# Four graph layers in one kernel: where the work at two layer borders is placed

## The chip, the cores and the metric

The kernel runs on one core of one Trainium2 chip. The metric is the device time of one execution in microseconds (us). Three runs of the kernel before took 2089.14, 2089.81 and 2091.94 us; their median, 2089.81 us, is the time before. A separate execution was recorded by the hardware profiler, and all durations of single instructions come from it.

The engines are called as the profile calls them: PE is TensorE (PEld its weight loads), ACT is ScalarE, DVE is VectorE, POOL is GpSimd, SP is SyncE. Each works through its own queue in order, and they wait for one another by semaphores.

## The reference

`x` has the shape (16, 1024, 64): 16 batches, 1024 nodes, 64 features. `adj` is a 1024 x 1024 graph that all batches and layers share. Four layers follow each other, each with a residual and a layer norm:

```python
x = layernorm(x + L0(x, W0, a0, adj))      # graph attention, one head
x = layernorm(x + L1(x, w0, b0, wa, ba, adj))
x = layernorm(x + L2(x, adj, W2, a2))      # graph attention, one head
x = layernorm(x + L3(x, adj, Wh, bh, Wo, bo, gamma, beta))   # dot-product attention, 4 heads and an outer one

# L0 and L2
h = x @ W;  s1 = h @ a1;  s2 = h @ a2
e = leaky_relu(s1[:, :, None] + s2[:, None, :], 0.2), masked by adj
out = elu(softmax(e, axis=2) @ h)

# L1: a softmax over the neighbours for each feature
feat = softplus(x * w0 / sqrt(2) + b0);  s = feat * wa + ba
out[i, d] = sum_j softmax_j(s[j, d], masked by adj[i, j]) * feat[j, d]
```

## The kernel before

The function `fast_path` does the work; `general_path` is a slower way that is run only if a test at the end of the data's range asks for it. The nodes lie on the 128 partitions, in 8 chunks; `xg[g]` holds four batches, so there are four groups g of four batches.

**Layers 0 and 2** are written by the same function, `gat_layer`. A pair of batches is prepared together: `prep_x` transposes x on PE (tile pxT) and copies it to SBUF on ACT (xT, line 920), `prep_s` multiplies it with w4 to the scores ps (line 926), `prep_top` copies them (l_s), takes their maximum on DVE (top) and over the partitions on POOL (gtop, line 937), `prep_p` makes two bounds (down, up) and two exponentials p and q on ACT, `prep_G` makes pg by matmuls (line 960) and its exponential G on ACT (line 961), and `prep_v` scales the values (vals) on ACT. Then a batch has eight units: one DVE instruction each makes e out of G, q and the graph aT (line 980), and PE multiplies e with vals (line 992; in layer 0 also line 1004, the sums u). A batch's ending is `evict` (yT, ysum), `project` (po, lines 1024 or 1032 and 1036), `divide` (v, and m = exp(v) at line 1061), `residual` (lines 1066, 1067), `norm` (statistics bn, line 1075, and for the second batch of a pair `moments`), `root`, `shift` and `store` (line 780). What belongs to which unit of which batch is written out by hand in `places` and `ends`; inside `gat_layer` the order of the instructions is the program's (`tc.manual_schedule`). The endings that fall past the last batch's fifth unit after the end are returned as a list, `ending`.

**Layer 1** works on groups. `prep_l1(g, q)` prepares half q of group g: the feature f and the exponent t on ACT and DVE, a transpose pf, a transpose back pe (line 1570), and hi and lo, the two halves of the exact product (lines 1572 to 1579: hi is a cast on ACT, lo the rest, on DVE). `product_l1` makes, for each of the eight chunks of nodes, 16 matmuls of aR (the graph, cast from aT at line 1666) with hi and lo into po, one PSUM bank of two (line 1642). `average` divides (lines 1652 to 1660: two steps on ACT, four on DVE) and takes statistics (line 1662). After a group's eight products come its moments; their root, shift and rows are put into the next group by the list `last`. Here the order is not fixed by hand: a scheduler orders each engine's queue when the kernel is built.

The two borders of the change are these. Between layers 0 and 1, a loop of four turns casts aR, finishes the halves of group 0 (`back` and `weighted` for both q), and puts the first three endings of layer 0's last batch into the turns:

```python
for i, task in enumerate([l1_tasks[q][-2 + i] for q in range(2) for i in range(2)]):
    for k in range(2 * i, 2 * i + 2):
        (nc.scalar.copy if k % 2 else nc.vector.tensor_copy)(aR[:, k, :], aT[:, k, :])
    for todo in [task] + ending[i : i + 1] * (i < 3):
        todo()
last = ending[3:]
```

Between layers 1 and 2, the pools of layer 1 are closed, layer 2's are opened, and the nine tasks that prepare layer 2's first pair (prep_x twice, prep_s twice, prep_top, prep_p, prep_G twice, prep_v) are called by `first` ahead of the first unit.

Of the kernel before, what the change touches and what calls it, by code (L numbers as in the profile page):

```python
# [8 lines left out]
F32 = mybir.dt.float32  # L9
# [3 lines left out]
AF = mybir.ActivationFunctionType  # L13
# [3 lines left out]
P = 128  # L17
FLT_MAX = 3.4028234e38
LN_EPS = 1e-5
ALPHA = 0.2  # L20
# [17 lines left out]
LAG = 2  # L38
# [544 lines left out]
def fast_path(  # L583
# [24 lines left out]
    nc = tc.nc  # L608
    B, N, D = x.shape
    C = N // P  # L610
# [4 lines left out]
    NG = B // GB  # L615
    HALF = N // 2
    CH = C // 2
# [58 lines left out]
    def catch_up():  # L676
        for task in [soon.pop(0) for _ in range(len(soon))]:
            task()
# [113 lines left out]
    def behind(step, lag):  # L792
        waiting.append(step)
        while len(waiting) > lag:
            waiting.pop(0)()

    def drain():
        while waiting:
            waiting.pop(0)()
# [97 lines left out]

        return [turn, scores] + [others, project] * zero_mean

    def gat_layer(w, name, zero_mean, extra, first, own, ordered):  # L900

        run = ExitStack()
        w1, w4, ind, s12, sums, w_out = (w[k] for k in ("w1", "w4", "ind", "s12", "sums", "out"))
        F = D - 1 if zero_mean else D
        pool = gp
        xT, G, pq, vals, only, stats = {}, {}, {}, {}, {}, {}
        if not zero_mean:
            ring = [pool.tile([P, C, 32], F32, tag=f"only{r}", name=f"only{r}", bufs=1) for r in range(3)]  # L910
            for t in ring:
                nc.gpsimd.memset(t, 0.0)

        def prep_x(b, h):
            if h == 0:
                xT[b] = pool.tile([P, N], F32, tag="xT", name=f"xT_{name}_{b}")
            pt = ps_t.tile([P, CH, P], F32, tag="t", name="pxT")
            for j in range(CH):
                nc.tensor.transpose(pt[:, j, :], x_pair(b, h * CH + j), ident)
            nc.scalar.copy(xT[b][:, h * HALF : (h + 1) * HALF], pt.rearrange("p j q -> p (j q)"))  # L920

        def prep_s(b, chunks):
            if 0 in chunks:
                pq[b] = ps_t.tile([P, HALF], F32, tag="t", name="ps12")
            for c in chunks:
                nc.tensor.matmul(
                    pq[b][:, 4 * c : 4 * c + 4], xT[b][:, c * P : (c + 1) * P], w4, start=True, stop=True
                )

        def prep_top(b):  # L930
# [19 lines left out]
            nc.scalar.activation(q, s2, AF.Exp, bias=up, scale=ALPHA - 1.0)  # L950
            pq[b] = (p, q, up)

        def prep_G(b, h):
            if h == 0:
                G[b] = pool.tile([P, 2, N], F32, tag="G", name=f"G_{name}_{b}")
            pg = ps_g.tile([P, 2, HALF], F32, tag="g", name="pg")
            cols = slice(h * HALF, (h + 1) * HALF)
            for i in range(2):
                rows = slice(i * D, (i + 1) * D)
                nc.tensor.matmul(pg[:, i, :], w1[rows, :], xT[b][rows, cols], start=True, stop=True)  # L960
            nc.scalar.activation(G[b][:, :, cols], pg, AF.Exp, bias=pq[b][2], scale=1.0 - ALPHA)  # L961

        def prep_v(b):
            p = pq[b - b % 2][0][:, :, b % 2]
            v = pool.tile([P, C, D], F32, tag="vals", name=f"vals_{name}_{b}", bufs=3)
            for c in range(C):
                nc.scalar.activation(v[:, c, :F], xb(b)[:, c, :F], AF.Copy, scale=p[:, c : c + 1])
            if zero_mean:
                nc.scalar.copy(v[:, :, F], p)
            else:  # L970
                only[b] = ring[b % 3]
                nc.scalar.copy(only[b][:, :, 0], p)
            vals[b] = v

        def attention(b):
            held = {}

            def unit(k):
                e = pool.tile([P, N], F32, tag="e", name="e", bufs=7 if zero_mean else 10)
                nc.vector.scalar_tensor_tensor(  # L980
                    e, G[b - b % 2][:, b % 2, :], pq[b - b % 2][1][:, k, b % 2 : b % 2 + 1], aT[:, k, :],
                    ALU.max, ALU.mult,
                )
                return e
# [24 lines left out]
            def evict():  # L1009
                y = ep.tile([P, HALF], F32, tag="y", name=f"yT_{name}_{b}")  # L1010
                nc.scalar.copy(y, held["y"])
                t = y
                if not zero_mean:
                    t = pool.tile([P, HALF], F32, tag="ysum", name=f"ysum_{name}_{b}")
                    nc.scalar.copy(t, held["t"])
                held["s"] = (y, t)

# [78 lines left out]
        slots = {}  # L1096

        def at(t, k, task):
            slots.setdefault((t, k), []).append(task)
# [15 lines left out]
        for b in range(0, B, 2):  # L1115
# [10 lines left out]
            for task, (t, k) in zip(chain, places):  # L1126
# [3 lines left out]
                    at(0, 0, task)  # L1130
                else:
                    ahead.append(task)
        for (t, k), todo in extra.items():
            for task in todo:
                at(t, k, task)
        first(ahead)
        if ordered:
            run.enter_context(tc.manual_schedule(engines=in_order))
        for t in range(B + 1):
            for k in range(C):  # L1140
                catch_up()
                if t < B:
                    unit, product, _ = work[t]
                    e = unit(k)
                    behind(lambda product=product, k=k, e=e: product(k, e), LAG if zero_mean else 2 * LAG)
                elif t == B and k == 0:
                    drain()
                if t < B or (t == B and k < own):
                    for task in slots.get((t, k), []):
                        task()  # L1150
        run.close()

        return [task for t in range(B, B + 3) for k in range(C) for task in slots.get((t, k), []) if (t, k) >= (B, own)]

# [431 lines left out]
    with tc.tile_pool(name="ps_g", bufs=1, space=bass.MemoryType.PSUM, reuse_waits="tile") as ps_g, tc.tile_pool(  # L1588
# [35 lines left out]
        for q, todo in enumerate(l1_tasks):  # L1624
            t = 7 + 2 * q
            places = (t, 0), (t, 2), (t, 4), (t, 6), (t + 2, 2), (t + 2, 7), (t + 3, 5)
            for place, task in zip(places, todo):
                extra.setdefault(place, []).append(task)
        ending = gat_layer(w_0, "l0", False, extra, first, 5, True)

    with tc.tile_pool(name="l1", bufs=2, reuse_waits="tile") as pool, tc.tile_pool(
        name="ps_l", bufs=2, space=bass.MemoryType.PSUM, reuse_waits="tile"
    ) as ps_l:
        l1["halves"] = pool
        l1["psum"] = lambda name: ps_l.tile([P, C, P], F32, tag="l", name=name)
        aR = pool.tile([P, C, N], F32R, tag="aR", name="aR", bufs=1)
# [12 lines left out]
        def average(g, ic, po, st):  # L1649
# [11 lines left out]
            for b in range(GB):  # L1661
                nc.vector.bn_stats(st[:, ic * GB + b, :], y[:, b, :])

        for i, task in enumerate([l1_tasks[q][-2 + i] for q in range(2) for i in range(2)]):
            for k in range(2 * i, 2 * i + 2):
                (nc.scalar.copy if k % 2 else nc.vector.tensor_copy)(aR[:, k, :], aT[:, k, :])
            for todo in [task] + ending[i : i + 1] * (i < 3):
                todo()
        last = ending[3:]
        for g in range(NG):  # L1670
            ahead = [[] for _ in range(C)]
            for q in range(2 if g + 1 < NG else 0):

                for ic, task in zip((q, q, q, q, q + 1, q + 2, q + 2, q + 4, q + 5), prep_l1(g + 1, q)):
                    ahead[ic].append(task)
            st = pool.tile([P, C * GB, 6], F32, tag="st1", name=f"st{g}")
            for ic in range(C):
                po = product_l1(g, ic)
                average(g, ic, po, st)
                for task in ahead[ic] + last[ic : ic + 1]:  # L1680
                    task()
            y = xg[g].rearrange("p c b d -> p (c b) d")
            mo = {}

            root, finish = moments(st)

            def shift(mo=mo, end=finish):
                mo["n"] = end()

            def rows(c, y=y, mo=mo):  # L1690
                scaled(y, y, mo["n"], range(c * 8, c * 8 + 8))

            last = [root, shift] + [lambda c=c, rows=rows: rows(c) for c in range(C * GB // 8)]
# [16 lines left out]
    def at(b, j, task, where=slots):  # L1710
        where.setdefault((b, j), []).append(task)
# [31 lines left out]
    for b in range(0, B, 2):  # L1743
        for t, j, task, where in (
# [14 lines left out]
            else:  # L1759
                at(b + t, j, task, where)  # L1760

    with tc.tile_pool(name="ps_g", bufs=1, space=bass.MemoryType.PSUM, reuse_waits="tile") as ps_g, tc.tile_pool(
        name="ps_p", bufs=1, space=bass.MemoryType.PSUM, reuse_waits="tile"
    ) as ps_p, tc.tile_pool(
        name="gat2", bufs=2, reuse_waits="tile"
    ) as gp:
        places = [(15, j) for j in (0, 1, 2, 3, 4, 5, 6, 7)]
        extra = {p: [task] for p, task in zip(places, ahead)}
        for p, task in zip(((0, 0), (0, 1), (0, 3), (0, 7), (1, 3), (1, 7)), last):
            extra.setdefault(p, []).append(task)  # L1770

        def first(ahead):
            for task in ahead:
                task()

        ending = gat_layer(later["w2"], "l2", True, extra, first, 5, True)
    for j, task in enumerate(ending):
        at(0, j, task)

# [125 lines left out]
```

## Time and profile before

| what | value |
|---|---|
| runs | 2089.14, 2089.81, 2091.94 us; median 2089.81 us |
| the profiled execution | 2090.28 us, of it the span from the first to the last instruction 2088.5 us |
| mean clock granted to TensorE | 0.977 of full speed |
| busy share of the span | PE 94%, DVE 87%, ACT 60%, PEld 41%, POOL 3% |
| layer 1's first product starts at | 295.63 us |
| layer 2's first unit starts at | 444.11 us |

Times inside the profile count from the span's start. A timeline's line has the start, the time, the engine, the line of the kernel with the operation, the written tile and the read ones, their shapes and the number of instructions taken together; in brackets stands how long the engine was idle before it and what ended that. A line of a group has busy time and mean ns, then the idle time ahead of the group's instructions and what ended most of it. A line of windows has, for a stretch of time, its length, each engine's busy time and instructions, the granted clock, the share of the DMA engines and GB/s.

### The profile page before, as it was taken

Reading aid. Unit: us, or ns where it says so; the run is one execution under the profiler, and the core shown is the slowest. Engines: PE = TensorE matmul, PEld = TensorE weight load, DVE = VectorE, ACT = ScalarE, POOL = GpSimd, SP = SyncE. Lnnn points to the kernel's source line nnn. Section 1 sums busy time; section 2 is a strip of 40 time slices with the busy share of each in tenths; the row PEclk is TensorE's granted clock in tenths of the full one; section 3 lists DMA queues with packets and bytes.
Section 4 is the critical chain, followed back from the end, with each engine's and each line's share of the span. In section 5 each row is a group of like instructions: output and inputs, shape, how many; then the busy total and the mean of one; then the engine's idle time right before and its main releaser. Section 6 shows DMA issues by size and latency. Waiting matters only on the chain.

```text
span 2088.5 us, 26441 instructions
## 1 busy us (share of the span) xinstructions
PE 1965.1 (94%) x10001; PEld 853.0 (41%) x10001; DVE 1820.0 (87%) x3197; ACT 1261.6 (60%) x2097; POOL 70.0 (3%) x77
## 2 busy tenths in 40 slices
PE   7999989998888999999999999999999999999983
PEld 4444347843332343334443434334343434433431
DVE  5899988879999777889898898988989989889997
ACT  4466568664556766566656656655665666665631
POOL 0000000000000000000000000000000000000001
PEclk9999999999999999999999999999999999999997
DMA  6000000000000200000000000000000000000000
GB/s 168 1 1 1 1 1 1 1 1 1 0 1 10 71 1 1 1 1 6 1 6 6 1 6 6 1 6 1 6 6 1 6 0 6 6 1 6 1 5 16
DMA packets 23655, 18.89 MB, mean 9 GB/s; under 512 B 19361, under 2 KB 19426, under 8 KB 23522
## 3 DMA queue, kind: packets, MB, share of 16 engines
q1 hardware_dynamic: 23218, 17.11, 2.8%
q8 instruction: 80, 1.31, 0.3%
q14 instruction: 53, 0.43, 0.1%
q10 hardware_dynamic: 304, 0.03, 0.0%
HBM read 12.95 MB, written 4.19 MB: 8 GB/s over the span
## 4 chain that ended last, share of the span: by engine, by line
PE 45%; DVE 39%; ACT 12%; issue 3%; SPq 0%; DMA 0%; POOL 0%; DVEq 0%; POOLq 0%; ACTq 0%
DVE e L1311 12%; PE y L1318 11%; PE s L1303 8%; DVE e L980 7%; ACT e L1307 6%; PE y_l L992 6%; DVE junk L1413 4%; PE po L1642 4%; DVE e L1424 4%; PE u_l L1004 3%; PE po L1333 2%; PE y L1433 2%; ACT e L1408 2%; DVE v L1343 2%; DVE z L786 1%
## 5 line engine op out<-in xcount | busy, mean ns | idle before, releaser
L1307 ACT ACTIVATE e<-s,shift 128x1024 f32<-128x1024 f32 x512 | 542.4, 1118 | 335.3 <-PE s L1303 334.4
L1311 DVE TENSOR_TENSOR e<-e,aT 128x1024 f32<-128x1024 f32 x512 | 600.4, 1217 | 1.9 <-ACT e L1307 1.8
L1318 PE MATMUL y<-e,vals 128*64 128x512 f32 x2048 | 490.0, 600 | 10.4 <-DVE e L1311 5.3
L1303 PE MATMUL s<-hT 64*128 64x512 f32 x2048 | 495.1, 603 | 1.2 <-ACT e L1307 0.9
L980 DVE SCALAR_TENSOR_TENSOR e<-G_l,q,aT 128x1024 f32<-128x1024 f32 x256 | 315.8, 1277 | 7.4 <-ACT G_l L961 7.3
L1303 PEld LDWEIGHTS s<-hT 64*128 64x128 f32 x2048 | 185.7, 186 | 278.0 <-issue 137.9
L992 PE MATMUL y_l<-e,vals_l 128*64 128x512 f32 x1024 | 262.8, 637 | 22.8 <-DVE e L980 22.0
L1318 PEld LDWEIGHTS y<-e,vals 128*64 128x64 f32 x2048 | 135.0, 137 | 277.4 <-issue 190.0
L1413 DVE SCALAR_TENSOR_TENSOR junk<-e,aN 128x1024 bf16<-128x1024 f32 x128 | 155.8, 1217 | 0.0
L1424 DVE TENSOR_TENSOR e<-e,aT 128x1024 f32<-128x1024 f32 x120 | 147.0, 1225 | 6.4
L1408 ACT ACTIVATE e<-s,shift 128x1024 f32<-128x1024 f32 x128 | 141.9, 1116 | 0.2 <-PE s L1403 0.2
L1403 PE MATMUL s<-h2T 64*128 64x512 f32 x512 | 130.7, 591 | 0.0
L992 PEld LDWEIGHTS y_l<-e,vals_l 128*64 128x64 f32 x1024 | 65.2, 142 | 160.4 <-issue 75.0
L1433 PE MATMUL y<-e,h2v 128*64 128x512 f32 x480 | 124.3, 596 | 0.7 <-DVE e L1424 0.7
L1642 PE MATMUL po<-hi,aR 128*128 128x512 f32 x256 | 102.8, 403 | 13.6 <-ACT hi L1578 8.6
L1642 PE MATMUL po<-lo,aR 128*128 128x512 f32 x256 | 101.2, 396 | 0.0
L780 ACT ACTIVATE x<-m,bn_shift,bn_rstd 128x64 f32<-128x64 f32 x256 | 88.5, 429 | 2.4 <-DVE bn_shift L771 2.4
L1246 POOL PARTITION_ALL_REDUCE gtop<-top x48 | 42.4, 884 | 1371.0 <-DVE top L1244 1269.2
L1333 PE MATMUL po<-wb,yT 128*128 128x130 f32 x512 | 74.2, 288 | 10.0 <-ACT e L1307 9.4
L1333 PEld LDWEIGHTS po<-wb,yT 128*128 128x128 f32 x512 | 61.9, 190 | 47.4 <-ACT e L1307 45.8
L1403 PEld LDWEIGHTS s<-h2T 64*128 64x128 f32 x512 | 49.9, 186 | 60.0 <-issue 27.4
L1337 DVE COPY sums<-po 128x8 f32<-128x8 f32 x64 | 10.8, 169 | 71.8 <-PE po L1333 71.8
(228 smaller groups left out, 2046.6 us busy)
## 6 DMA issues: line engine op xcount, KB each, us to landing
adj<-in_adj_dram SPq DMA_DIRECT2D x16, 512.0 KB, 4.1
x<-in_x_dram SPq DMA_DIRECT2D x16, 256.0 KB, 5.2
out_dram<-res SPq DMA_DIRECT2D x16, 256.0 KB, 2.0
wl<-in_L_gnn_Wh_dram SPq DMA_DIRECT2D x2, 64.0 KB, 3.4
wo<-in_L_gnn_Wo_dram SPq DMA_DIRECT2D x1, 64.0 KB, 3.0
l_wd<-in_L_gnn_W_dram ACTq DMA_DIRECT2D x2, 16.0 KB, 4.6
l_wd<-in_L_gnn_W_dram SPq DMA_DIRECT2D x2, 16.0 KB, 2.0
bo<-in_L_gnn_bo_dram SPq DMA_DIRECT2D x1, 32.0 KB, 3.0
```

The costliest lines, as they stand in the source:

```text
L980: nc.vector.scalar_tensor_tensor(e, G[b - b % 2][:, b % 2, :], pq[b - b % 2][1][:, k, b % 2 : b % 2 + 1], aT[:, k, :], ALU.max, ALU.mult,)
L992: nc.tensor.matmul(held["y"][h * D : (h + 1) * D, :], vals[b][:, k, :], e[:, h * HALF : (h + 1) * HALF], start=(k == 0), stop=(k == C - 1),)
L1303: nc.tensor.matmul(s[:, i, :], hT[rows, k * P : (k + 1) * P], hT[rows, cols], start=True, stop=True)
L1307: nc.scalar.activation(e, s, AF.Exp, bias=shifts[b, n])
L1311: nc.vector.tensor_tensor(e, e, bc_mid(aT[:, k, h * HALF : (h + 1) * HALF], 2), ALU.mult)
L1318: nc.tensor.matmul(held[h][i * D : (i + 1) * D, :], vals[b][:, k, :], e[:, i, :], start=(k == 0), stop=(k == C - 1),)
L1333: nc.tensor.matmul(o[:, j // 2, j % 2, :], held["y"][:, j * P : (j + 1) * P], wb[:, n, :], start=True, stop=True,)
L1403: nc.tensor.matmul(s[:, i, :], hT[rows, (i + k // CH) % 2, k % CH * P : (k % CH + 1) * P], hT[rows, 0, :], start=True, stop=True,)
L1408: nc.scalar.activation(e, s, AF.Exp, bias=shifts[b])
L1413: nc.vector.scalar_tensor_tensor(junk.rearrange("p c q -> p (c q)").bitcast(BF16), e.rearrange("p i q -> p (i q)"), 1.0, aN[:, k, :], ALU. ...
L1424: nc.vector.tensor_tensor(m, e, aT[:, k, :].rearrange("p (i q) -> p i q", i=2), ALU.mult)
L1642: nc.tensor.matmul(po.rearrange("p q k f -> p (q k f)"), aR[:, k, ic * P : (ic + 1) * P], e[:, k].rearrange("p q k f -> p (q k f)"), start ...
```

## The change

It has two parts.

At the border of layers 0 and 1, only layer 0's `project` is called ahead of the loop of four turns; `divide`, `residual` and what follows go into `last`, that is, into the tasks of group 0's eight products.

At the border of layers 1 and 2, the first pair's tasks are made ahead of layer 1. `prep_G` is split into `scores_G` (the matmuls) and `exps_G` (the exponentials). The first eight tasks (prep_x twice, prep_s twice, prep_top, prep_p, scores_G twice) are put into group 3 of layer 1, the last group; in place of layer 2's own tiles, xT takes two buffers of the pool ep (tag "v"), and pg layer 1's two PSUM buffers. The exponentials and vals are called when layer 1's SBUF pool is closed, and only then is its PSUM pool closed. Since the scheduler orders layer 1's queues, a task can land earlier than it is called.

```diff
-    def gat_layer(w, name, zero_mean, extra, first, own, ordered):
+    def gat_layer(w, name, zero_mean, own, room=None):
...
         def prep_x(b, h):
             if h == 0:
-                xT[b] = pool.tile([P, N], F32, tag="xT", name=f"xT_{name}_{b}")
+                if room and b == 0:
+                    xT[b] = room["xT"]()
+                else:
+                    t = gp.tile([P, N], F32, tag="xT", name=f"xT_{name}_{b}")
+                    xT[b] = [t[:, i * HALF : (i + 1) * HALF] for i in range(2)]
...
-        def prep_G(b, h):
-            if h == 0:
-                G[b] = pool.tile([P, 2, N], F32, tag="G", name=f"G_{name}_{b}")
-            pg = ps_g.tile([P, 2, HALF], F32, tag="g", name="pg")
-            cols = slice(h * HALF, (h + 1) * HALF)
+        def scores_G(b, h):
+            pg = room["g"]() if room and b == 0 else ps_g.tile([P, 2, HALF], F32, tag="g", name="pg")
             for i in range(2):
                 rows = slice(i * D, (i + 1) * D)
-                nc.tensor.matmul(pg[:, i, :], w1[rows, :], xT[b][rows, cols], start=True, stop=True)
-            nc.scalar.activation(G[b][:, :, cols], pg, AF.Exp, bias=pq[b][2], scale=1.0 - ALPHA)
+                nc.tensor.matmul(pg[:, i, :], w1[rows, :], xT[b][h][rows, :], start=True, stop=True)
+            pgs[b, h] = pg
+
+        def exps_G(b, h):
+            if h == 0:
+                G[b] = gp.tile([P, 2, N], F32, tag="G", name=f"G_{name}_{b}")
+            cols = slice(h * HALF, (h + 1) * HALF)
+            nc.scalar.activation(G[b][:, :, cols], pgs[b, h], AF.Exp, bias=pq[b][2], scale=1.0 - ALPHA)
...
+        if room:
+            ahead[-3:-1] = [lambda f=f, h=h: f(0, h) for f in (scores_G, exps_G) for h in range(2)]
...
+    l2_ahead, l2_go = gat_layer(later["w2"], "l2", True, 5, room=dict(
+        xT=lambda: [ep.tile([P, C, D], F32, tag="v", name="xT").rearrange("p c d -> p (c d)") for _ in range(2)],
+        g=lambda: l1["psum"]("pg").rearrange("p (i c) q -> p i (c q)", i=2),
+    ))
...
+        ending[0]()
         for i, task in enumerate([l1_tasks[q][-2 + i] for q in range(2) for i in range(2)]):
             for k in range(2 * i, 2 * i + 2):
                 (nc.scalar.copy if k % 2 else nc.vector.tensor_copy)(aR[:, k, :], aT[:, k, :])
-            for todo in [task] + ending[i : i + 1] * (i < 3):
-                todo()
-        last = ending[3:]
+            task()
+        last = ending[1:]
         for g in range(NG):
...
+            if g + 1 == NG:
+                for ic, task in zip((1, 2, 3, 3, 4, 5, 6, 6), l2_ahead):
+                    ahead[ic].append(task)
...
+    gat = ExitStack()
+    gp = gat.enter_context(tc.tile_pool(name="gat2", bufs=2, reuse_waits="tile"))
+    for task in l2_ahead[8:]:
+        task()
+    l1_psum.close()
...
-        def first(ahead):
-            for task in ahead:
-                task()
-
-        ending = gat_layer(later["w2"], "l2", True, extra, first, 5, True)
+        ending = l2_go(extra)
```

More of the change, by code (lines that the diff above doesn't have):

```diff
@@ L898, in gat_setup @@
         return [turn, scores] + [others, project] * zero_mean
-    def gat_layer(w, name, zero_mean, extra, first, own, ordered):
-        run = ExitStack()
+    def gat_layer(w, name, zero_mean, own, room=None):
         w1, w4, ind, s12, sums, w_out = (w[k] for k in ("w1", "w4", "ind", "s12", "sums", "out"))
         F = D - 1 if zero_mean else D
-        pool = gp
-        xT, G, pq, vals, only, stats = {}, {}, {}, {}, {}, {}
+        xT, G, pgs, pq, vals, only, stats = {}, {}, {}, {}, {}, {}, {}
         if not zero_mean:
-            ring = [pool.tile([P, C, 32], F32, tag=f"only{r}", name=f"only{r}", bufs=1) for r in range(3)]
+            ring = [gp.tile([P, C, 32], F32, tag=f"only{r}", name=f"only{r}", bufs=1) for r in range(3)]
             for t in ring:
@@ L919, in prep_x @@
                 nc.tensor.transpose(pt[:, j, :], x_pair(b, h * CH + j), ident)
-            nc.scalar.copy(xT[b][:, h * HALF : (h + 1) * HALF], pt.rearrange("p j q -> p (j q)"))
+            nc.scalar.copy(xT[b][h], pt.rearrange("p j q -> p (j q)"))
         def prep_s(b, chunks):
@@ L926, in prep_s @@
                 nc.tensor.matmul(
-                    pq[b][:, 4 * c : 4 * c + 4], xT[b][:, c * P : (c + 1) * P], w4, start=True, stop=True
+                    pq[b][:, 4 * c : 4 * c + 4], xT[b][c // CH][:, c % CH * P : (c % CH + 1) * P], w4,
+                    start=True, stop=True,
                 )
@@ L951, in prep_p, with prep_G @@
             pq[b] = (p, q, up)
-        def prep_G(b, h):
-            if h == 0:
-                G[b] = pool.tile([P, 2, N], F32, tag="G", name=f"G_{name}_{b}")
-            pg = ps_g.tile([P, 2, HALF], F32, tag="g", name="pg")
-            cols = slice(h * HALF, (h + 1) * HALF)
+        def scores_G(b, h):
+            pg = room["g"]() if room and b == 0 else ps_g.tile([P, 2, HALF], F32, tag="g", name="pg")
             for i in range(2):
                 rows = slice(i * D, (i + 1) * D)
-                nc.tensor.matmul(pg[:, i, :], w1[rows, :], xT[b][rows, cols], start=True, stop=True)
-            nc.scalar.activation(G[b][:, :, cols], pg, AF.Exp, bias=pq[b][2], scale=1.0 - ALPHA)
+                nc.tensor.matmul(pg[:, i, :], w1[rows, :], xT[b][h][rows, :], start=True, stop=True)
[5 more added lines that the diff above has]
+            nc.scalar.activation(G[b][:, :, cols], pgs[b, h], AF.Exp, bias=pq[b][2], scale=1.0 - ALPHA)
+        def prep_G(b, h):
+            scores_G(b, h)
+            exps_G(b, h)
         def prep_v(b):
             p = pq[b - b % 2][0][:, :, b % 2]
-            v = pool.tile([P, C, D], F32, tag="vals", name=f"vals_{name}_{b}", bufs=3)
+            v = gp.tile([P, C, D], F32, tag="vals", name=f"vals_{name}_{b}", bufs=3)
             for c in range(C):
@@ L978, in unit @@
             def unit(k):
-                e = pool.tile([P, N], F32, tag="e", name="e", bufs=7 if zero_mean else 10)
+                e = gp.tile([P, N], F32, tag="e", name="e", bufs=7 if zero_mean else 10)
                 nc.vector.scalar_tensor_tensor(
@@ L1013, in evict @@
                 if not zero_mean:
-                    t = pool.tile([P, HALF], F32, tag="ysum", name=f"ysum_{name}_{b}")
+                    t = gp.tile([P, HALF], F32, tag="ysum", name=f"ysum_{name}_{b}")
                     nc.scalar.copy(t, held["t"])
@@ L1132, in gat_layer, with go @@
                     ahead.append(task)
[L1133 to L1149, printed above, removed]
-                        task()
-        run.close()
-        return [task for t in range(B, B + 3) for k in range(C) for task in slots.get((t, k), []) if (t, k) >= (B, own)]
+        if room:
+            ahead[-3:-1] = [lambda f=f, h=h: f(0, h) for f in (scores_G, exps_G) for h in range(2)]
+        def go(extra):
+            for (t, k), todo in extra.items():
+                for task in todo:
+                    at(t, k, task)
+            with tc.manual_schedule(engines=in_order):
+                for t in range(B + 1):
+                    for k in range(C):
+                        catch_up()
+                        if t < B:
+                            unit, product, _ = work[t]
+                            e = unit(k)
+                            behind(lambda product=product, k=k, e=e: product(k, e), LAG if zero_mean else 2 * LAG)
+                        elif t == B and k == 0:
+                            drain()
+                        if t < B or (t == B and k < own):
+                            for task in slots.get((t, k), []):
+                                task()
+            return [
+                task for t in range(B, B + 3) for k in range(C) for task in slots.get((t, k), []) if (t, k) >= (B, own)
+            ]
+        return ahead, go
     whT = const.tile([P, HD], F32, tag="whT", name="whT")
@@ L1628, in fast_path @@
                 extra.setdefault(place, []).append(task)
[L1629 to L1633, printed above, removed]
+        ahead, go = gat_layer(w_0, "l0", False, 5)
+        first(ahead)
+        ending = go(extra)
+    l2_ahead, l2_go = gat_layer(later["w2"], "l2", True, 5, room=dict(
+        xT=lambda: [ep.tile([P, C, D], F32, tag="v", name="xT").rearrange("p c d -> p (c d)") for _ in range(2)],
+        g=lambda: l1["psum"]("pg").rearrange("p (i c) q -> p i (c q)", i=2),
+    ))
+    l1_psum = ExitStack()
+    ps_l = l1_psum.enter_context(tc.tile_pool(name="ps_l", bufs=2, space=bass.MemoryType.PSUM, reuse_waits="tile"))
+    with tc.tile_pool(name="l1", bufs=2, reuse_waits="tile") as pool:
         l1["halves"] = pool
@@ L1760, in fast_path @@
                 at(b + t, j, task, where)
+    gat = ExitStack()
+    gp = gat.enter_context(tc.tile_pool(name="gat2", bufs=2, reuse_waits="tile"))
+    for task in l2_ahead[8:]:
+        task()
+    l1_psum.close()
     with tc.tile_pool(name="ps_g", bufs=1, space=bass.MemoryType.PSUM, reuse_waits="tile") as ps_g, tc.tile_pool(
         name="ps_p", bufs=1, space=bass.MemoryType.PSUM, reuse_waits="tile"
-    ) as ps_p, tc.tile_pool(
-        name="gat2", bufs=2, reuse_waits="tile"
-    ) as gp:
+    ) as ps_p:
         places = [(15, j) for j in (0, 1, 2, 3, 4, 5, 6, 7)]
@@ L1770, in fast_path @@
             extra.setdefault(p, []).append(task)
-        def first(ahead):
-            for task in ahead:
-                task()
-        ending = gat_layer(later["w2"], "l2", True, extra, first, 5, True)
+        ending = l2_go(extra)
+    gat.close()
     for j, task in enumerate(ending):
```

## The prediction

> **What bounds the kernel now.** First the page: its span, and the group of layer 0's and layer 2's attention units (line 980, one VectorE instruction per unit).
>
> ```profile
> span 2088.5 us, 26441 instructions
> PE 1965.1 (94%) x10001; PEld 853.0 (41%) x10001; DVE 1820.0 (87%) x3197; ACT 1261.6 (60%) x2097; POOL 70.0 (3%) x77
> L980 DVE SCALAR_TENSOR_TENSOR e<-G_l,q,aT 128x1024 f32<-128x1024 f32 x256 | 315.8, 1277 | 7.4 <-ACT G_l L961 7.3
> ```
>
> The last column matters: in 256 units VectorE stood idle for 7.4 us only, nearly all of it behind ScalarE's G. Layer 2 is thus VectorE's: what makes its first unit earlier makes everything after it earlier by the same amount, as the order behind it is unchanged. Second, the timeline of VectorE from layer 1's last product to that first unit:
>
> ```profile
> 433.81 0.42 DVE L1655 TENSOR_TENSOR t<-po,r 128x256 f32<-128x256 f32 x1 [1.18 <-ACT r L1653]
> ...
> 437.19 0.19 DVE L704 TENSOR_TENSOR most_var<-most_var,bn_var 128x32 f32<-128x32 f32 x1
> 437.43 0.19 DVE L933 COPY l_s<-ps 128x32 f32<-128x32 f32 x1
> 437.66 0.17 DVE L935 TENSOR_REDUCE top<-l_s 128x1 f32<-128x16 f32 x1
> 438.38 0.15 DVE L943 TENSOR_SCALAR down<-gtop 128x1 f32<-128x1 f32 x1 [0.55 <-POOL gtop L937]
> ...
> 444.11 2.48 DVE L980 SCALAR_TENSOR_TENSOR e<-G_l,q,aT 128x1024 f32<-128x1024 f32 x2 [5.52 <-ACT G_l L961]
> ```
>
> The last product ends at 432.92 (the chain of waits has it there), so this border is 11.19 long: 4.4 of layer 1's own end (two ScalarE steps, the average, the moments), and 6.8 of pair 0's preparation. Third, the timeline of the other border, from layer 0's end to layer 1's first product:
>
> ```profile
> 289.14 0.63 ACT L1061 ACTIVATE m<-v 128x512 f32<-128x512 f32 x1
> 289.67 1.03 ACT L1578 CAST hi<-f 128x1024 fp32r<-128x1024 f32 x1
> ...
> 294.54 1.04 ACT L1578 CAST hi<-f 128x1024 fp32r<-128x1024 f32 x1
> 295.48 1.06 ACT L1536 ACTIVATE t<-t 128x1024 f32<-128x1024 f32 x1
> ```
>
> ScalarE works here without a break; the first product starts at 295.63, when the second of these casts is done. Fourth, TensorE between the borders. It has five idle stretches there (0.2, 1.8, 1.8 and 1.2 us, apart from the first of 8.6), and from 400.02 to 432.92 none: group 3 is TensorE's, 3.62 us for each of eight products.
>
> ```profile
> 398.47 0.39 PE L1642 MATMUL po<-lo,aR 128*128 128x512 f32 x1
> 400.02 0.47 PE L1642 MATMUL po<-hi,aR 128*128 128x512 f32 x1 [1.17 <-DVE t L1657]
> ...
> 434.30 1.06 PE L926 MATMUL ps<-l_w,xT_l 128*128 128x4 f32 x8 [1.39 <-ACT xT_l L920]
> ...
> 460.40 1.13 PE L960 MATMUL pg<-xT_l,l_w 64*128 64x512 f32 x4
> 461.46 1.94 PE L992 MATMUL y_l<-e,vals_l 128*64 128x512 f32 x8
> ```
>
> **Part 1, layer 0's last ending.** In the changed program's order ScalarE has m (line 1061) no longer ahead of the last hi cast but four instructions behind it. Everything from x's scaling at 283.68 to that cast follows without idle time, and m held ScalarE for 289.67 - 289.14 = 0.53. The cast then starts at 294.0. What it needs from VectorE (line 1573 on the second half) started at 292.93 and took 1.21; ahead of it residual's two instructions go (0.6 each from start to start), but the wait for the first hi cast, which now comes at 290.1 instead of 289.67, takes 0.4 back, so it ends near 293.5, in time. The transposes of pe now stand behind line 1036's matmuls: done near 286.9, needed at 287.29. So the first product starts 0.54 earlier, and the products follow each other.
>
> What is moved (residual 0.68 + 0.69, eight statistics 1.11, moments some 0.9: 3.4 on VectorE, 0.53 on ScalarE) lies beside the first two products: VectorE was idle for 4.33 before 304.21 there, ScalarE for 1.02 before 302.85. Without this cover it would delay the first average by 3.4. The later stalls of TensorE (1.8 at 334.89 and at 365.95) come out of stretches that start from a wait for a product, and these keep their order, so I carry 0.54 through. Its bounds, -1.0 and 2.0, come from the clock rows below.
>
> **Part 2, layer 2's first pair.** Its ps, top, p, q and pg go into groups 2 and 3. It is not free, for TensorE takes most of it in line with the products:
>
> - Between group 2's products 6 and 7 now stand both halves of ps and the first half of pg. The row at 434.30 is one half of ps: 8 records, the next instruction 0.99 later; two are 1.98. A half of pg is four records, at 460.40, 1.06 to the next. Together 3.04, and they fill the stall of 1.16 that ended at 400.02: product 7 starts 1.88 later, with part 1's 0.54 still to be taken off.
> - The second half of pg stands before group 3's last product: 1.06, uncovered.
> - ScalarE's copies of xT (two, 1.05) go to about 369, where ScalarE then waits 2.73 for the next product. p and q (0.6) fall into its wait of 4.05 before 403.93.
> - l_s, top, down, up (0.65) go into VectorE's queue at about 401 to 404, with a new wait for the all-reduce on POOL; behind it stands line 1657 of product 6, whose PSUM buffer group 3's first product needs. The all-reduce took 0.35 at 438.00 with VectorE idle and 1.24 in most other rows (1.37 at most). VectorE waits 0.15 to 1.2 and frees the buffer between 403.7 and 404.8; product 7 ends at 405.0. So nothing is lost; without that cover it would be up to 1.2.
> - Two buffers of ep's "v" hold xT, and layer 1's two PSUM buffers pg: their former readers were done at 302 and 399.5.
>
> The last product therefore ends at 432.92 - 0.54 + 1.88 + 1.06 = 435.32. From there ScalarE needs 0.76 to the start of G's first half and 1.1 for each half: 2.9, within VectorE's 4.38 (437.30 - 432.92) to the end of the moments. So what is late next is VectorE itself, and the first unit starts at 439.7 instead of 444.11: 4.4 earlier. vals (2.2 on ScalarE, done at 5.1 after the product) comes before the first unit is finished (5.6). The root of the last moments and xT of pair 2 follow, in time for line 712 two units later.
>
> **The clock.** The profile's windows over TensorE's restart at each border:
>
> ```profile
> 297.00:299.00 2.00, 2.00 (x5) 1.63 (x6) 1.86 (x13) 2.00 (x3) 0.00 (x0) 0.50 0.00 0
> 301.00:302.00 1.00, 1.00 (x5) 0.80 (x4) 0.00 (x0) 0.83 (x1) 0.00 (x0) 0.66 0.00 0
> 446.00:448.00 2.00, 2.00 (x6) 0.42 (x4) 1.90 (x6) 0.59 (x2) 0.00 (x0) 0.50 0.00 0
> 448.00:450.00 2.00, 1.91 (x10) 0.41 (x8) 2.00 (x3) 2.00 (x7) 0.00 (x0) 0.89 0.00 0
> ```
>
> (The number before the last two is the granted clock.) Layer 1 ran at half clock for 6.0 us, which cost 3.0; an idle time of about 7.2 instead of 8.6 keeps that, so I take no change. In layer 2 TensorE will be idle for some 4.5 between its transposes and the first unit, and start at half clock again; there VectorE hides it, since units came without a pause from 447.29 on.
>
> [...]
>
> From the rows alone the bounds are these: the other border's restart took 3.0 (445.45 to about 448.4) against 6.0 here. Half of that difference is 1.5, so a luckier phase makes part 1 0.54 + 1.5 = 2.0, and one that is as much unluckier 0.54 - 1.5 = -1.0.
>
> **The sum.** The profiled execution took 2090.28 for its span of 2088.5; the median of the three runs is 2089.81, 0.47 less. 2090.28 - 4.4 = 2085.9; on the median, 2085.4. About 0.2% (4.2 us) is what a measurement of this kernel can tell from no change, so the forecast lies at the edge.
>
> **The rivals.**
> - *Less comes through.* Part 1's 0.54 is lost in VectorE's busy stretch before 334.89, and TensorE's 1.16 stall reappears behind the new matmuls: 6.8 - 3.04 - 1.06 = 2.7, so 2087.1, no change. A clock that rises 1.5 later would leave about as much, 2.9. For it: VectorE had no idle time from 326 to 343. Against it: pg needs nothing from VectorE later than 394.65.
> - *More comes through.* With the clock's 1.5: 5.9, so 2083.9. For it: the idle time ahead of the products gets shorter; against it: it stays above the time after which the clock was at half here (from 287.0 to about 291.5).
> - *Slower, by TensorE's clock in layer 2.* At half clock a unit's matmuls take 1.98 (445.45), VectorE's unit 1.24. Seven e buffers hide five units of delay, thus some 13 units; from there each costs 0.74. To turn 4.4 into a loss of 4.2 needs 12 more: some 45 us at half clock after the border. Price then: 2094. Against it: the half-clock stretch of this border is some 10 us (438.2 to 448.4).
> - *It doesn't do what it says.* If G's space had to wait for the average's last tile (2.7 after the product instead of 0.76), the first unit would come at 4.9: 0.5 less gained, 2085.9. In the changed order G has no such wait.
>
> **How the numbers follow.** Forecast 0.68, with its own range of 3.4 to 5.4 us gained (2084.4 to 2086.4); of it 0.42 lies beyond 4.2. Less 0.12, more 0.14, slower 0.06; the last rival is inside the forecast's range. Faster 0.42 + 0.14 = 0.56, same 0.26 + 0.12 = 0.38, slower 0.06. The range goes from 5.9 gained to 2.7 gained, each widened by the 0.7 by which the lowest run before lies under the median: 2083.2 to 2087.8.
>
> **What would show it.** Right: TensorE's first product at 295.1; no idle time before group 2's product 7, but ps and pg; the last product's end at 435.3; the first unit at 439.7, with VectorE waiting for nothing before it. Wrong: an all-reduce that holds line 1657 and then TensorE; G later than the moments; VectorE idle behind matmuls in layer 2; a first product no earlier.

## The result and the profile after

Before: 2089.82 us (median of 22 runs, those of the front among them). After: 2084.17 us (22 runs). The ratio is 0.9976, 95% interval 0.9970 to 0.9983, or 5.0 us less (3.6 to 6.3). The forecast was 2085.4 in a range of 2083.2 to 2087.8, "faster" its likeliest side. The interval excludes no change; it contains the 4.2 us that the prediction drew as its line, so it does not settle on which side of that line the gain lies.

In the changed program lines have moved: a unit is line 991, G 968, pg 961, ps 929, m 1072; layer 1's product is line 1665, the hi cast 1594, the average 1675 to 1685. The page first.

```profile
span 2084.4 us, 26441 instructions
...
L991 DVE SCALAR_TENSOR_TENSOR e<-G_l,q,aT 128x1024 f32<-128x1024 f32 x256 | 315.8, 1276 | 2.1 <-ACT G_l L968 2.1
```

The units cost the same 315.8, but VectorE waited 2.1 for them instead of 7.4: G is no longer what the first one waits for. The timeline of VectorE at layer 2's border:

```profile
436.74 0.42 DVE L1678 TENSOR_TENSOR t<-po,r 128x256 f32<-128x256 f32 x1 [2.50 <-PE pxT L922]
...
440.14 0.19 DVE L704 TENSOR_TENSOR most_var<-most_var,bn_var 128x32 f32<-128x32 f32 x1
440.25 1.28 DVE L991 SCALAR_TENSOR_TENSOR e<-G_l,q,aT 128x1024 f32<-128x1024 f32 x1
```

The unit of 440.25 has no bracket: the moments end and it starts. TensorE's timeline shows what that cost, behind product 6 of group 2 and ahead of the last product:

```profile
398.50 0.39 PE L1665 MATMUL po<-lo,aR 128*128 128x512 f32 x1
398.73 1.84 PE L929 MATMUL ps<-l_w,xT 128*128 128x4 f32 x16
400.50 1.13 PE L961 MATMUL pg<-xT,l_w 64*128 64x512 f32 x4
401.56 0.50 PE L1665 MATMUL po<-hi,aR 128*128 128x512 f32 x1
...
430.52 0.39 PE L1665 MATMUL po<-lo,aR 128*128 128x512 f32 x1
430.84 1.13 PE L961 MATMUL pg<-xT,l_w 64*128 64x512 f32 x4
431.89 0.50 PE L1665 MATMUL po<-hi,aR 128*128 128x512 f32 x1
...
435.68 1.04 PE L922 MATMUL pxT<-ident,x 128*128 128x128 f32 x8
441.67 4.91 PE L1003 MATMUL y_l<-e,vals_l 128*64 128x512 f32 x13 [4.96 <-ACT bn_rstd L708]
```

Where before product 7 had the stall of 1.16, ps and pg now stand without a gap. The stalls of 0.20, 1.81 and 1.79 in groups 0 and 1 are unchanged. At the other border ScalarE's last cast starts at 294.46 behind one activation of group 1, without m:

```profile
293.32 1.25 ACT L1549 ACTIVATE t<-x,b,c 128x1024 f32<-128x1024 f32 x1
294.46 1.04 ACT L1594 CAST hi<-f 128x1024 fp32r<-128x1024 f32 x1
```

Layers 0 and 3, whose code is the same in all kernels here, differ by up to 3.7 and 3.0 us from one profile to the next. So I count from layer 0's last ysum copy (its start on ScalarE) on. These are the two ends of the first stretch, before and after:

```profile
283.20 0.59 ACT L1015 COPY ysum_l<-u_l 128x512 f32<-128x512 f32 x1 [1.08 <-PE u_l L1004]
295.63 0.80 PE L1642 MATMUL po<-hi,aR 128*128 128x512 f32 x1 [8.62 <-ACT hi L1578]
...
283.64 0.59 ACT L1026 COPY ysum_l<-u_l 128x512 f32<-128x512 f32 x1 [1.07 <-PE u_l L1015]
295.56 0.79 PE L1665 MATMUL po<-hi,aR 128*128 128x512 f32 x1 [7.29 <-ACT hi L1594]
```

| from, to | before | after |
|---|---|---|
| last ysum copy to layer 1's first product | 12.43 | 11.92 |
| first product to the end of the last product | 137.28 | 140.28 |
| end of the last product to layer 2's first unit | 11.20 | 4.41 |
| together | 160.91 | 156.61 |
| first unit to the end of layer 2's last unit | 220.79 | 220.80 |

All of the difference that the profile can locate, 4.30, lies between these borders, and layer 2 passes it on whole. The runs' 5.0 (3.6 to 6.3) holds it.

### The profile page after: what moved, and what is told of

The parts are those of the page before. It is cut to its first block, busy times and chain, and to the rows that moved or that the text cites. A ratio compares the mean times of both kernels' runs of the same rounds, so it can differ in the third digit from the quotient of the medians.

```text
span 2084.4 us, 26441 instructions
## 1 busy us (share of the span) xinstructions
PE 1963.2 (94%) x10001; PEld 852.4 (41%) x10001; DVE 1820.0 (87%) x3197; ACT 1262.0 (61%) x2097; POOL 70.4 (3%) x77
## 3 DMA queue, kind: packets, MB, share of 16 engines
q8 instruction: 81, 1.33, 0.3%
## 4 chain that ended last, share of the span: by engine, by line
PE 47%; DVE 39%; ACT 11%; issue 3%; DMA 0%; POOL 0%; SPq 0%; DVEq 0%; POOLq 0%; ACTq 0%
DVE e L1327 12%; PE y L1334 11%; PE s L1319 8%; DVE e L991 7%; ACT e L1323 6%; PE y_l L1003 6%; PE po L1665 5%; DVE junk L1429 4%; DVE e L1440 4%; PE u_l L1015 3%; PE po L1349 2%; PE y L1449 2%; ACT e L1424 2%; DVE v L1359 2%; DVE z L786 1%
## 5 line engine op out<-in xcount | busy, mean ns | idle before, releaser
L991 DVE SCALAR_TENSOR_TENSOR e<-G_l,q,aT 128x1024 f32<-128x1024 f32 x256 | 315.8, 1276 | 2.1 <-ACT G_l L968 2.1
```

Of the source, the lines that this page charges most:

```text
L991: nc.vector.scalar_tensor_tensor(e, G[b - b % 2][:, b % 2, :], pq[b - b % 2][1][:, k, b % 2 : b % 2 + 1], aT[:, k, :], ALU.max, ALU.mult,)
```

## The experiments

The theory: part 2 brings the gain, 6.8 at the border less some 2.9 of matmuls in the products' line; part 1 brings half a microsecond; layer 2 hides its half clock. The rivals: part 1 or the clock does it; the uncovered pg isn't uncovered; layer 2 pays for the cold start.

**Part 1 alone.** The old program with layer 0's endings moved:

```diff
+        ending[0]()
         for i, task in enumerate(...):
...
-            for todo in [task] + ending[i : i + 1] * (i < 3):
-                todo()
-        last = ending[3:]
+            task()
+        last = ending[1:]
```

> Part 1 alone (layer 0's last divide, residual and norm behind the halves; layer 2's pair as before). My theory: the m activation was the only thing that left ScalarE's unbroken chain, so layer 1's first product comes 11.9 us after the start of ysum's copy instead of 12.4, and the stretch from that product to layer 2's first unit stays at 148.5; in time 0.5 us less than before, which a few runs cannot tell from nothing. Rival (the moved 3.4 us of VectorE delay group 0): the first product is earlier too, but the stretch to layer 2's first unit grows by 0.5 to 3.4, and nothing or less than nothing is gained.

Measured: 2090.95 against 2089.28, ratio 1.0008 (0.9998 to 1.0017). The first product came 11.90 after the ysum copy, 0.53 earlier, as the theory has it. No gain shows in the time: the interval goes from 0.4 less to 3.6 more. In the profiled execution TensorE was at half clock (0.50 granted) for only some 3.3 us after the first product, and the products took 136.02 instead of 137.28. Yet the clock fell to 0.50 again within pair 0's preparation, which the old order still has behind the last product, 2.4 us after TensorE's restart there (before the change 3.9 us after it):

```profile
432.02 1.06 PE L926 MATMUL ps<-l_w,xT_l 128*128 128x4 f32 x8 [1.39 <-ACT xT_l L920]
433.01 1.12 PE L960 MATMUL pg<-xT_l,l_w 64*128 64x512 f32 x2
434.06 1.52 PE L926 MATMUL ps<-l_w,xT_l 128*128 128x4 f32 x8
435.51 2.07 PE L960 MATMUL pg<-xT_l,l_w 64*128 64x512 f32 x2
```

The first halves of ps and pg took 1.06 and 1.12, the second ones, of the same work, 1.52 and 2.07, and the border took 12.02 instead of 11.20. From the first product to layer 2's first unit that is 148.04 against 148.48, so the rival (VectorE's moved work delays group 0) has no support; all three stretches together are 159.95 against 160.91. So part 1's half microsecond exists, and is smaller than what the clock's timing gives and takes in one execution. That part 1 caused the fall is not shown.

**Part 2 alone.** The changed program with the old loop of four turns (the diff above, the other way).

> Part 2 alone (layer 2's first pair in layer 1's last groups; the border of layers 0 and 1 as before). My theory: first product 12.4 us after ysum's copy starts, the stretch from first to last product grows from 137.3 by 3.04 + 1.06 - 1.16 = 2.9, and the first unit follows the last product after 4.4 instead of 11.2: 3.9 us less than before. Rival (part 2 needs part 1, or more of it is hidden): a growth of the product stretch of under 2 us, and 5 us or more gained.

Measured: 2084.73 (9 runs), ratio 0.9981 (0.9971 to 0.9991), 4.0 less. First product at 12.44, border 2 at 4.40, together 156.26 in its profile, 4.65 less than before: part 2 is the gain. The stretch of the products grew by 2.15, not by the 2.9 of the theory. The clock accounts for that: in this profile the half clock ended 4.57 after the first product, before the change 6.05 after it, and half of the difference, 0.74, makes it 2.89. Against the changed kernel, whose half clock ended 6.51 after the first product, that is worth some 1.0, more than part 1; so the profile of part 2 alone is 0.35 shorter than that of the whole change.

**Full clock at layer 1's start.** The changed program with matmuls that keep TensorE busy through the border:

```diff
         last = ending[1:]
+        idle = ps_t.tile([P, HALF], F32, tag="t", name="idle")
+        for i in range(31):
+            nc.tensor.matmul(idle, ident16, aT[:, 0, :HALF], start=(i == 0), stop=(i == 30))
```

> The changed kernel with 31 added bf16 matmuls (128x512, some 0.22 us each at full clock, 6.7 together) that nobody reads, put on TensorE between the transposes of pe and layer 1's first product, where it is idle for 7.3 us. My theory: the half clock after the idle time is what costs 3 us at this border, so the first 16 products take 0.23 us each instead of 0.43 and the last product comes 2.5 to 3 us earlier. Rival 1 (ScalarE and VectorE are just as late in group 0, so the clock is hidden): TensorE at full clock, but it waits for them, and under 1 us is gained. Rival 2 (the added matmuls hold the queue): the first product is later than 11.9 after ysum's copy, and the time is the same or worse.

Measured: 2084.57 (7 runs), ratio 0.9978 (0.9966 to 0.9990), not to be told from the changed kernel's. TensorE's timeline in its profile:

```profile
284.44 6.85 PE L1694 MATMUL idle<-aT,ident 128*128 128x512 bf16 x31
291.89 0.73 PE L1665 MATMUL po<-hi,aR 128*128 128x512 f32 x2 [0.59 <-ACT hi L1594]
293.15 0.50 PE L1665 MATMUL po<-lo,aR 128*128 128x512 f32 x1 [0.53 <-DVE lo L1595]
```

The granted clock was 1.00 from the added matmuls to the last product, and first to last product took 138.58, 1.70 less. That is under the 2.5 to 3 I expected: at full clock TensorE meets VectorE's lo (0.53) and, at 301.70, f (0.55). The half clock of some 6.5 us, at 0.50 granted, costs 3.2 in matmuls by estimate; about half of that is not gained. The two new waits make 1.08 of it, which the half clock had hidden; the rest is not located.

**The second half of pg twice.** The changed program, each of that half's matmuls issued twice.

> The changed kernel with the second half of the pair's scores (pg ahead of the last product) computed twice, the same values. My theory: TensorE is the bound of group 3 and nothing covers this work, so the last product and layer 2's first unit come later by one more half, 0.9 to 1.1 us, and the stretch from the last product to the first unit stays 4.4. Rival (the moved matmuls lie in slack): no change of the first unit.

Measured, one run: 2090.41, and this group in TensorE's timeline:

```profile
431.97 1.99 PE L962 MATMUL pg<-xT,l_w 64*128 64x512 f32 x8
433.89 0.50 PE L1666 MATMUL po<-hi,aR 128*128 128x512 f32 x1
```

1.92 from start to start instead of 1.05, and from the restart after the stall of 1.79 to the last product's end 70.72 instead of 69.88: 0.84 more, a little under the 0.9 expected, and all of it uncovered. From ysum to the first unit this profile is 2.48 longer; 1.6 of that is something else (the last section has it), and the rest of the longer time lies outside these borders.

**The second half of pg behind the last product.**

```diff
-                for ic, task in zip((1, 2, 3, 3, 4, 5, 6, 6), l2_ahead):
+                for ic, task in zip((1, 2, 3, 3, 4, 5, 6), l2_ahead):
...
-    for task in l2_ahead[8:]:
+    for task in l2_ahead[7:]:
```

> The changed kernel, but the second half of pg is computed after layer 1's last product instead of ahead of it. It tells whether that half's 1.06 lies uncovered in the line of products, as the sum has it. My theory: TensorE is idle behind the last product and ScalarE has its two steps there (0.76), then G's first half (1.1), so the second half's matmuls are done at +1.1, in time for G's second half at +1.9. The last product comes 0.9 to 1.1 earlier after the stall of 1.79 (69.9 becomes 68.9), the first unit stays at +4.4, and the time falls by 1.0, to 2083.2. Rival: the matmuls fall into something late (a half clock, the transposes of pair 2 behind them), and what is gained comes back at the border: the first unit at +5.4, 2084.2.

```profile
431.88 1.13 PE L961 MATMUL pg<-xT,l_w 64*128 64x512 f32 x4
432.94 1.09 PE L922 MATMUL pxT<-ident,x 128*128 128x128 f32 x8
437.78 5.70 PE L1003 MATMUL y_l<-e,vals_l 128*64 128x512 f32 x16 [3.75 <-ACT bn_rstd L708]
```

In its profile the half now fills idle time of TensorE (3.75 is left of 4.96), the border stays 4.40, and restart to last product's end is 68.55, 1.33 less. The runs, 2084.25 (ratio 0.9977, 0.9967 to 0.9987), don't resolve it; 2083.2 was expected.

**No cold start in layer 2.** 20 matmuls of the same kind as above, ahead of layer 2's first unit, into a tile that nothing reads.

> The changed kernel with 20 more matmuls of the graph (128x512, bf16, some 0.21 each, 4.3 us) after layer 1's last product, into a tile that nothing reads: TensorE goes through the border into layer 2 without its 4.96 us of idle time. It tells whether the half clock at layer 2's start costs anything (the rival of the prediction that would end slower). My theory: VectorE hides it, so the granted clock is 1.00 in the stretch and the time stays: the first unit at +4.4 after the last product, layer 2 220.8 long, 2084.2 within 1.0. Rival: the half clock costs some of it: layer 2 gets shorter by 0.7 or more.

```profile
431.51 4.49 PE L1794 MATMUL idle<-aT,ident 128*128 128x512 bf16 x20
435.83 1.04 PE L922 MATMUL pxT<-ident,x 128*128 128x128 f32 x8
437.50 2.18 PE L1003 MATMUL y_l<-e,vals_l 128*64 128x512 f32 x8 [0.62 <-ACT bn_rstd L708]
440.58 2.27 PE L1003 MATMUL y_l<-e,vals_l 128*64 128x512 f32 x8 [0.90 <-DVE e L991]
```

The clock was 1.00 from 430 to 446, and TensorE, now fast, waits for VectorE's e at once (0.90). The first unit came at +4.40, layer 2 took 220.91 against 220.80, the time was 2083.31 (ratio 0.9973, 0.9962 to 0.9983). The cold start costs nothing here, and the rival that would have ended slower falls.

**ScalarE's casts of aR on POOL.** `nc.scalar.copy` becomes `nc.gpsimd.tensor_copy` in the loop of four turns.

> The changed kernel, but the four odd casts of aR go to POOL instead of ScalarE. It tells whether ScalarE's chain really is what layer 1's first product waits for. My theory: it is. Four casts of 1.05 (0.94 from start to start) leave ScalarE's chain, but VectorE's own chain had only 0.26 + 1.17 + 0.48 + 0.44 = 2.35 of idle time there, and the built order puts m and one more activation of group 1 ahead of the last hi cast again (0.53 + 1.06). So the first product comes 1 to 2.3 us earlier, 9.6 to 10.9 after layer 0's last ysum copy instead of 11.92, and the time falls by about 1.5, to 2082.7. Rival: POOL's casts become the last: the nearest rows of POOL (a memset of 256 elements in 0.315) put one of 1024 elements at about 0.9 or more, and four one after the other while VectorE is busy could take 8 or longer, and slow VectorE's own casts (0.69); then the first product comes at +11.9 or later, and the time is equal or up to 2 more.

Measured: 2084.2 (6 runs), ratio 0.9975 (0.9961 to 0.9988), the changed kernel's time and not the 2082.7 expected. The first product came at 10.79, 1.13 earlier: ScalarE's chain was what it waited for. But here are VectorE's casts in the changed kernel, then those on VectorE and POOL in this one, and TensorE's start:

```profile
283.65 2.50 DVE L1690 CAST aR<-aT 128x1024 fp32r<-128x1024 bf16 x4 [1.59 <-PE u_l L1015]
...
280.88 5.03 DVE L1690 CAST aR<-aT 128x1024 fp32r<-128x1024 bf16 x4 [1.59 <-PE u_l L1015]
280.97 5.83 POOL L1690 CAST aR<-aT 128x1024 fp32r<-128x1024 bf16 x4 [56.59 <-PE u_l L1015]
...
291.67 1.22 PE L1665 MATMUL po<-hi,aR 128*128 128x512 f32 x2 [6.17 <-ACT hi L1594]
...
293.85 0.80 PE L1665 MATMUL po<-lo,aR 128*128 128x512 f32 x1 [0.96 <-DVE lo L1595]
```

VectorE's own four casts, 2.5 in the changed kernel, took 5.03 beside POOL's: 2.53 more, which uses up the 2.35 of idle time that VectorE had there. TensorE then waits 0.96 for its lo. At TensorE's restart behind the stall of 1.81, 0.96 of the 1.13 is gone (40.33 after the first product, 39.37 in the changed kernel). So most of what ScalarE saved, VectorE gave back; the half clock, which lasted 1.1 longer here, has a share in that which this run does not separate. Behind that stall the clock fell to 0.50 in this profile (the last section).

**Three of these together**: POOL's casts, 22 matmuls ahead of layer 1 and the second half of pg behind the last product.

> The changed kernel with three things together: the odd casts of aR on POOL, 22 matmuls into an unread tile ahead of layer 1's first product, so that it starts at full clock (31 of them brought 1.70 alone), and the second half of pg after the last product. Theory: the three lie one behind the other and add up: 1.5 + 1.7 + 1.0 = 4.2 less, 2080.0. Rival: an earlier and faster start only meets VectorE's and ScalarE's work of group 0 (with full clock alone two new waits of 0.5 came up on TensorE), so that the first two share a bound: 2.7 less, 2081.5; and if POOL's casts are late, they take away 1.5 or more: 2083.

Measured: 2079.26 (4 runs), ratio 0.9949 (0.9933 to 0.9966), better than both kernels; its interval lies clear of the changed kernel's. From ysum to the first unit it took 152.62, 3.99 less than the changed kernel, with full clock in all of border 1. It is 2.28 less than with full clock alone, of which 1.33 is the late half of pg; the other 0.95 is left to POOL's casts, which were not tried with full clock alone. So the sum of the theory (4.2, 2080.0) nearly holds and the rival's 2.7 doesn't, but the shares are others than expected: the late half brings more than 1.0, and what is left to POOL's casts is less than 1.5. Behind its first two matmuls TensorE now waits 1.45 for VectorE's lo, with full clock alone 0.53.

## Why the prediction was right, step by step

- **Part 1: 0.54 on the first product.** Measured 0.51 to 0.52 in the changed kernel, 0.53 alone. What was moved (m, residual, statistics) was covered: behind the first product no stall is new, and the stalls of 1.81 and 1.79 follow it as before. But "I carry 0.54 through" can't be seen in the time; the clock's timing is larger (0.74 between the profiles before and of part 2 alone).
- **Part 2: 1.88 ahead of product 7.** It was 1.53 (restart to product 7's start: 35.60 against 34.07). Both halves of ps took 1.77, not 1.98; and the stall was worth more than the 1.16 in its bracket: start to start, 398.47 to 400.02 is 1.55 where a matmul in line takes 0.23, so 1.32 was free. 1.77 + 1.06 - 1.32 = 1.51.
- **The second half of pg: 1.06 uncovered.** Uncovered, yes, but 1.39 (product 7's start to the last product's end: 34.28 against 32.89). The step that was undersized is the price of cutting into the products: 430.52 to 431.89 is 1.37, 1.14 over a matmul's slot, and the matmul behind it takes 0.34 instead of 0.23. Moved away it gave 1.33. The two errors cancel, 2.92 in place of 2.94. Of the 1.39, 1.14 and 0.11 are these two; 0.14 is not located. That the total came out is luck: one piece was put 0.35 too high, the other 0.33 too low.
- **The all-reduce's wait, 0.15 to 1.2, covered.** The all-reduce took 0.43, near the lower end; VectorE waited 0.25, and the product behind it lost nothing:

```profile
402.53 0.42 DVE L1679 SCALAR_TENSOR_TENSOR r<-t,r 128x256 f32<-128x256 f32 x1
402.74 0.43 POOL L941 PARTITION_ALL_REDUCE gtop<-top  x1 [175.62 <-DVE top L939]
403.20 0.15 DVE L947 TENSOR_SCALAR down<-gtop 128x1 f32<-128x1 f32 x1 [0.25 <-POOL gtop L941]
```

- **The border: 4.38 behind the last product, G in time.** 4.41; G ran from 436.62 to 438.72, 1.5 ahead of need, so the rival of G waiting for space falls too:

```profile
436.62 2.10 ACT L968 ACTIVATE G_l<-pg,up 128x1024 f32<-128x1024 f32 x2
```

- **The clock.** Layer 1's half clock lasted some 6.5 us after the first product instead of 6.0, within the bounds. Their 1.5 either way was an estimate from two restarts of one profile (6.0 and 3.0), and nothing ahead of the runs showed that a phase sets it. In the runs, where no matmuls were added ahead of the first product, the half clock lasted from 3.3 (part 1 alone) to 7.6 (POOL's casts) after it. In layer 2 it was granted as follows, and hidden (the kernel with 20 more matmuls, at full clock there, has no shorter layer 2):

```profile
440.00:442.00 2.00, 0.33 (x2) 0.23 (x4) 1.97 (x4) 1.97 (x8) 0.00 (x0) 1.00 0.00 0
442.00:444.00 2.00, 2.00 (x7) 0.49 (x4) 1.90 (x6) 0.52 (x3) 0.00 (x0) 0.50 0.00 0
444.00:446.00 2.00, 2.00 (x9) 0.40 (x7) 2.00 (x3) 2.00 (x7) 0.00 (x0) 0.64 0.01 4
```

  It was at half for under 4 us, far from what the slower rival needed. That rival's 45 is itself too low: its 25 units of 1.98 make some 50.
- **The sum.** 4.4 forecast, 4.30 in the profile, 5.0 (3.6 to 6.3) in the runs. The first rival's 2.7 lies outside that interval. "More comes through" (5.9) lies inside it; the profile gives it no support, since its half clock was no shorter. By the profiles the forecast is right at both borders and in the total; that the runs' median lies 1.2 under 2085.4 is within their interval, and nothing located explains it.

## What to carry to other kernels

When preparation moves from a border into an earlier stage, count first what it costs there in line: here 6.8 left the border and 2.9 came back, and by the profiles half of that came from one piece that could have stayed, because TensorE was idle for 4.96 behind the last product anyway. Read a stall's worth from start to start against the normal slot, not from its bracket (here 1.32, not 1.16). And before half a microsecond is hunted, look at what varies by itself: a half clock that ended 4.57 after the first product in one profile and 6.05 after it in another is worth 0.74 by estimate, more than the 0.52 of part 1.

## What was not expected of the hardware

- **Behind a short stall the clock fell in two profiles of ten.** The stall of 1.81 in group 1 is in every profile. In eight of the ten shown here the clock stays at 1.00 behind it; in two (pg twice, POOL's casts) it drops to 0.50 for some 3.4 us, 1.3 and 1.4 us after TensorE's restart. Windows of the kernel with pg twice, where TensorE restarts at 334.45:

```profile
334.00:335.00 1.00, 0.55 (x3) 0.50 (x4) 1.00 (x3) 0.00 (x0) 0.00 (x0) 1.00 0.00 0
335.00:337.00 2.00, 2.00 (x8) 1.58 (x7) 1.97 (x9) 0.99 (x1) 0.00 (x0) 0.68 0.00 0
337.00:338.00 1.00, 1.00 (x4) 0.81 (x3) 0.93 (x3) 0.21 (x1) 0.00 (x0) 0.50 0.00 0
338.00:339.00 1.00, 1.00 (x3) 0.74 (x3) 0.93 (x7) 0.00 (x0) 0.00 (x0) 0.50 0.00 0
```

  From that restart to the next one the two took 32.65 and 32.68, the changed kernel 31.03: some 1.6 us lost. What decides between the two outcomes no run shows.
- **The restart's length varies, in steps.** After the first product the half clock lasted from some 3.3 us (part 1 alone) to 7.6 (POOL's casts, with a stall of 0.96 inside), at idle times of 6.2 to 8.6 us. The idle time does not order them: behind 8.62 it was 6.05 before the change and 4.57 with part 2 alone. Counted whole, from where the clock falls to where it rises in the windows, the half-clock stretch at this border is 10.24 us in six profiles (before, the change, part 2 alone, pg twice, POOL's casts, the late half of pg) and 6.8 with part 1 alone; with 20 more matmuls ahead of layer 2's first unit it is 13.24 from 284.00 on, where the windows begin. At layer 2's start the stretches are 3.4, 6.8 or 10.24. So in these profiles every stretch seen whole is about one, two or three times the shortest. In the six with 10.24 the half clock behind the first product still went from 4.57 to 7.6: they differ by where in the stretch the first product falls. This is the phase for which the prediction kept its 1.5.
- **VectorE's casts are slower beside POOL's.** In the changed kernel four casts of aR took VectorE 2.50, one of them 0.69. Beside POOL's four, which took 5.83 together, the same four took it 5.03. Why they are slower, and what POOL's take alone, no run shows.
